# Reordering the opening part of a two-layer conditioned expert kernel: small parameter steps first, some loads later, unread products on TensorE

## The chip, the cores and the metric

The kernel runs on one core of one Trainium2 chip. The metric is device time in microseconds, from one launch to its end. The kernel before took 1190.12 us (median of three runs: 1186.35, 1190.12 and 1195.05). One further execution was recorded by the hardware profiler, and every duration below is from it.

Engines are named as the profile names them: PE is TensorE (its weight loads are listed as PEld), DVE is VectorE, ACT is ScalarE, POOL is GpSimd, and SP is SyncE, which here only issues DMAs. A "q" behind a name (SPq, ACTq) is that engine's instruction queue.

## The reference

The input `x` has 8 sequences (the text calls each of them a batch, b0 to b7) of 512 tokens with 256 channels. Two layers are added to it one after the other.

```python
# layer 0: a small adapter chosen by the batch's language, then a layer norm
h = relu(x @ W1[lang] + b1[lang])                  # 256 -> 64
y = x + h @ W2[lang] + b2[lang]                    # 64 -> 256
c = norm(y) * gamma[lang] + beta[lang]
# layer 0: experts choose tokens
S = softmax(c @ Wg.T).swapaxes(1, 2)               # 8 experts
G, I = top_k(S, 128)                               # 128 of the 512 tokens, per batch and expert
out = G * (gelu(c[I] @ W1 + b1) @ W2 + b2)         # 256 -> 1024 -> 256
x = x + scatter_add(out, I)
# layer 1: causal running means with learned rates (tau) and blend weights, gates, a layer norm
# layer 1: 64 routed experts, 8 per token, and a shared expert; their sum is added to x
```

Two things of layer 1 matter here, because they depend on the parameters alone and not on `x`: the rates `alpha = 1 / (1 + exp(tau))` (9 numbers) and the softmax of the blend weights (256 x 8 numbers). They can be computed at any time before layer 1 begins.

## The kernel before

**How the order comes about.** The function `tile_adaln_ffn_kernel` does not emit instructions as it goes. It adds steps to an `Order`: each step has an engine, a guessed cost in us, a rank, the keys that it reads and writes, and a function that emits its instructions. `Order.run` then plays through these guesses (a table switch of ACT is guessed at 1.3 us, a DMA at 0.19 MB per us) and calls the steps' functions in the order so found; where several steps could begin within 0.25 us of each other, the lower rank goes first. On the chip only the order on each engine remains. Each engine works strictly through its own list, and an instruction waits only for the data and buffers that it really needs. So `after=` or a changed cost sets no wait on the chip: it moves a step in the list. A step that is late holds up everything behind it on its engine.

SP issues nearly all loads. A load on SP waits until the load eight places before it has landed; in the lists this stands as a wait on one of eight DMA semaphores used in turn.

**The opening part**, for each batch b, is `adapter(b)` (line 302):

- loads of the transposed rows (`load_xb`, line 312, tile `axb`, three buffers) and of the rows (`load_xt`, line 317, tile `axt`, three buffers), 512 KB each. For b0 and b1 the rows are loaded from ACT's queue, all others from SP's.
- gathers by POOL of the language's weights (`row_w1` line 324, `row_w2` line 331, tile `aw`, two buffers each) and gains (line 337).
- `down` (PE, line 357, two products of 512 columns), `relu` (ACT, line 360), `up` (PE, line 375, four products of 256 columns over 65 rows; for b2, b3 and b4 the rows themselves are added on PE through an identity, line 379).
- the sum (DVE line 384, or ACT line 390), its statistics (DVE lines 406 and 407, or ACT lines 428 and 434), a square root (ACT line 411 or 441), a reciprocal (DVE line 418 or 445), the norm (ACT line 456), a transposition (PE line 265, ACT line 280), the eight expert scores per token (PE line 472), and their copy (DVE line 481).

After b0 and b1 comes `choose(0)`: softmax, and then 16 rounds of three DVE instructions each (lines 542, 543 and 544), in which one chain of dependent instructions finds the best 128 tokens, eight at a time. Its lists (lines 552 to 573) are what the first experts wait for. `choose(1)` does the same for b2 to b7, later.

Then `expert(n)` runs 32 times (4 pairs of batches, 8 experts): a gather of the tokens (POOL line 612), transposition (PE line 625, ACT line 280), `up` (PE line 646), gelu (ACT line 656), `down` (PE line 713), and a scatter-add (POOL line 731). The weights of an expert are 2 MB (lines 593 and 598, two buffers each). Layer 1 follows pair by pair (`conditioning`, `route`), interleaved with the experts of the next pairs; then the shared expert, and the 64 routed experts.

**The parameter steps** are in `w_rates` (line 770): `less` (DVE 787, 788), `exp_tau` (ACT 773), `exp_blend` (ACT 791), `rates` (DVE 776 to 782) and `shares` (DVE 795 to 797), all of rank 95. Their inputs `taus` and `blend` are loaded in `w_load` (line 747) with the weights of layer 1, rank 30. ACT needs its "exp" table for them, and its "sqrt" table for the norms.

The lines that call these:

```python
nc.scalar.activation(root, eps, AF.Sqrt)           # line 1498: loads ACT's sqrt table
...
w_load()
w_rates()
```

Of the kernel before, what the change touches and what calls it, by code (L numbers as in the profile page):

```python
# [26 lines left out]
PAIR = 2 * 2 * (H // P) * F1 + 3 * H  # L27
FAR = 6
NEAR = 6
LATE = ()  # L30
EPS = 1e-5
NEG = -3.0e38
# [112 lines left out]
def kernel(ctx: ExitStack, tc: tile.TileContext, d: dict, out: bass.AP):  # L145
# [148 lines left out]
    groups = [GROUPS[0], [b for g in GROUPS[1:] for b in g]]  # L294
    lgs = [r0.tile([P, NC // 2, 2, len(g) * E0], F32, name=f"lg{i}") for i, g in enumerate(groups)]

    begun, last_adapter = [], []

    def small(name, shape):
        return r0.tile(shape, F32, name=name)  # L300
# [1 line left out]
    def adapter(b):  # L302
# [1 line left out]
        rank = b if early_one else 50 + b  # L304

        by_dve = early_one or b > 4
        hot = 1.0 if b else 1.7
        xb, xt, w1, w2, hT, xa, c0, c0T = ((k, b) for k in ("axb", "axt", "aw1", "aw2", "ahT", "axa", "ac0", "ac0T"))

        def load_xb():  # L310
# [2 lines left out]

        def load_xt():
            t = tile_of(xt, "axt", [P, NC, H])
            queue = nc.scalar if early_one else nc.sync
            queue.dma_start(out=t, in_=d["x"][b].rearrange("(c p) h -> p c h", p=P))

        def keep():
            nc.sync.dma_start(out=x1_rows[b].rearrange("(c p) h -> p c h", p=P), in_=V[xt])  # L320
# [22 lines left out]
            t = tile_of(hT, "ahT", [A + 1, S])  # L343
            nc.gpsimd.memset(t[A : A + 1, :], 1.0)

        load(512 * KB, load_xb, new=[(xb, "axb")], rank=b)
        load(512 * KB, load_xt, new=[(xt, "axt")], rank=b)
        pool(1.1, row_w1, new=[(w1, "aw1")], rank=rank - 3, lag=2.5)
        pool(1.1, row_w2, new=[(w2, "aw2")], rank=rank - 3, lag=2.5)
        pool(1.0, one, new=[(hT, "ahT")], rank=rank)  # L350
        pool(1.1, row_gains, w=[("gains", b)], rank=rank + 2, lag=2.5)

# [6 lines left out]
        def relu():  # L359
            nc.scalar.activation(V[hT][:A, :], V["ph", b][:A, :], AF.Relu, bias=V[w2][:A, H : H + 1])  # L360

        pe(2.0 * hot, down, r=[w1, xb, w2, hT], new=[(("ph", b), "mm")], rank=rank, after=() if early_one else begun)
        act(0.7, relu, r=[("ph", b), w2], w=[hT], rank=rank)

        sums = ("asum", b)
# [129 lines left out]
    def choose(g):  # L495
        n = len(groups[g])
        rank = 10 if g == 0 else 60
        lg = lgs[g]
        lgr = lg.rearrange("p q h (b e) -> p (q h b) e", e=E0)
        G, R = NC * n, n * E0  # L500
        K = ("choice", g)
        t = {}

        def less():
            t["mx"] = only([P, G], F32, name=f"mx{g}")
            nc.vector.tensor_reduce(t["mx"], lgr, AX.X, ALU.max)
            nc.vector.tensor_tensor(lgr, lgr, t["mx"].unsqueeze(2).to_broadcast([P, G, E0]), ALU.subtract)

        def exp():
            nc.scalar.activation(lgr, lgr, AF.Exp)  # L510

        def share():
            t["sm"] = only([P, G], F32, name=f"sm{g}")
            nc.vector.tensor_reduce(t["sm"], lgr, AX.X, ALU.add)
            nc.vector.reciprocal(t["sm"], t["sm"])
            nc.vector.tensor_tensor(lgr, lgr, t["sm"].unsqueeze(2).to_broadcast([P, G, E0]), ALU.mult)

        def turn():
# [12 lines left out]
        dve(0.8, less, r=[("lg", g, b) for b in groups[g]], w=[K], rank=rank)  # L531
        act(0.35, exp, w=[K], rank=rank, table="e")
        dve(0.9, share, w=[K], rank=rank)
        pe(0.7, turn, r=[K], new=[(("cpt", g), "mm")], rank=rank)
        s = dve(0.5, keep, r=[("cpt", g)], w=[K], rank=rank)
        if g == 0:
            begun.append(s)
        for i in range(K0 // 8):
            def one(i=i):
                prob, best, best_i = (t[k] for k in ("prob", "best", "best_i"))  # L540
                o = slice(8 * i, 8 * i + 8)
                nc.vector.max(best[:, o], prob)
                nc.vector.max_index(best_i[:, o], best[:, o], prob)
                nc.vector.match_replace(prob, best[:, o], prob, -1.0)

            dve(1.45, one, w=[K], rank=rank)


        def lists_of():
            t["lists"] = [only([2 * R, K0], F32, name=f"best{k}{g}") for k in "fbr"]  # L550
            for dst, src in zip(t["lists"], (t["best_i"], t["best_i"][:, ::-1], t["best"][:, ::-1])):
                nc.vector.tensor_copy(dst, src)

        def turn_lists():
            pt = bank(("clt", g))
            for k, src in enumerate((*t["lists"], t["best"])):
                nc.tensor.transpose(pt[:, 2 * R * k : 2 * R * (k + 1)], src, ident[: 2 * R, : 2 * R])

        def keep_lists():
            gT = r0.tile([P, R], F32, name=f"gT{g}")  # L560
            ix = r0.tile([P, R], I32, name=f"ix{g}")
            first_ones = only([P, R], F32, name=f"fo{g}")
            apart = only([P, R], F32, name=f"ap{g}")
            n1, n2, v2, v1 = (V["clt", g][:, R * k : R * (k + 1)] for k in (0, 3, 5, 6))
            held = only([P, 2, R], F32, name=f"hd{g}")
            nc.vector.tensor_copy(held[:, 0], n1)
            nc.vector.tensor_copy(held[:, 1], v1)
            nc.vector.tensor_tensor(first_ones, held[:, 1], v2, ALU.is_ge)
            nc.vector.tensor_tensor(gT, held[:, 1], v2, ALU.max)
# [15 lines left out]
    def expert(n):  # L585
# [16 lines left out]
        def load_3():  # L602
            nc.sync.dma_start(out=tile_of(b2, "fb2", [P, H]), in_=d["fb2"][e : e + 1, :].to_broadcast([P, H]))

        load(1024 * KB, load_1, new=[(w1, "fw1")], rank=20 + n)
        load(1024 * KB, load_2, new=[(w2, "fw2")], rank=20 + n)
        load(128 * KB, load_3, new=[(b2, "fb2")], rank=20 + n)

        which = 0 if bs[0] in groups[0] else 1
        for b in bs:  # L610
# [129 lines left out]

    W = {}

    def w_load():
        def one(name, shape, src, size):
            def fn():
                W[name] = wp.tile(shape, F32, name=name)
                nc.sync.dma_start(out=W[name], in_=src)
            load(size, fn, w=[name], rank=30)

        def one_w(name, k, n):  # L750
            one(name, [P, k // P, n], d[name].rearrange("(c p) n -> p c n", p=P), 4 * k * n)

        one("bn2", [D1, 1], d["bn2"], 32)
        one("cb", [P, 3, NH], d["cb"].rearrange("p (k c) -> p k c", k=3), 3 * KB)
        one("lgb", [P, 2 * NH], d["lgb"], 2 * KB)
        one("taus", [P, 1 + D1], d["taus"].to_broadcast([P, 1 + D1]), 4 * KB)
        one("blend", [P, NH, D1], d["blend"].rearrange("p (c k) -> p c k", c=NH), 8 * KB)
        one("wn2", [P, P], d["wn2"], 64 * KB)
        one("bn1", [P, 1], d["bn1"], 512)
        one_w("wn1", H, P)  # L760
        one_w("lwg", 2 * H, H)
        one_w("wsoma", H, H)
        one_w("wtemp", H, H)
        one_w("wout", H, H)
        one_w("rw", H, E1)
        one_w("wsgu", H, 2 * F1)
        one_w("wsd", 2 * P, H)

    def w_rates():
# [5 lines left out]
        def rates():  # L775
            nc.vector.tensor_scalar_add(W["alpha"], W["alpha"], 1.0)
            nc.vector.reciprocal(W["alpha"], W["alpha"])

            W["hb"] = wp.tile([P, 3, NH], F32, name="hb")
# [16 lines left out]
            nc.vector.reciprocal(W["bmx"], W["bmx"])  # L796
            nc.vector.tensor_tensor(bw, bw, W["bmx"].unsqueeze(2).to_broadcast([P, NH, D1]), ALU.mult)

        dve(0.5, less, w=["blend"], rank=95)
        act(0.3, exp_tau, r=["taus"], w=["alpha"], rank=95, table="e")  # L800
        act(0.3, exp_blend, w=["blend"], rank=95, table="e")
        dve(0.8, rates, r=["cb", "bn2"], w=["alpha", "hb"], rank=95)
        dve(0.8, shares, w=["blend"], rank=95)

        def ranks():
            nc.vector.tensor_copy(early, early_i)
            nc.vector.tensor_copy(early1, early1_i)

        dve(1.1, ranks, w=["early"], rank=96)

    ix_c1 = wp.tile([P, E1], I32, name="ix_c1")

# [682 lines left out]


    last_tokens = []
    nc.scalar.activation(root, eps, AF.Sqrt)
    load(8 * KB, lambda: nc.sync.dma_start(
        out=fwg, in_=d["fwg"].rearrange("(c p) e -> p c e", p=P)), w=["fwg"], rank=0.5)  # L1500
    for b in range(B):
# [7 lines left out]
    w_rates()  # L1509
    last_adapter += order.steps  # L1510
    for n in range(len(units)):
        expert(n)
# [93 lines left out]
```

## Time and profile before

| what | us |
|---|---|
| median of three runs | 1190.12 |
| profiled execution, its time | 1186.26 |
| profiled execution, its span | 1184.5 |
| PE busy (share of the span) | 1035.0 (87%) |
| DVE busy | 684.9 (58%) |
| ACT busy | 490.9 (41%) |
| POOL busy | 379.5 (32%) |
| first product of the program (PE line 357) | at 11.66 |
| first of the 16 rounds of `choose(0)` (DVE line 542) | at 42.58 |
| lists of `choose(0)` ready (DVE line 573) | at 69.52 |
| first transposition for an expert (PE line 625) | at 75.64 |

The profile gives, for a stretch of time, how long each engine was busy, and the clock granted to TensorE as a share of its full speed. [...] A wait is listed with the engine and line that waited, what ended the wait, the total in us, the number of waits, and the longest. The time between the span (1184.5 us) and the execution's own time (1186.26 us) is 1.8 us.

### The profile page before, as it was taken

The page shows a single profiled execution, that of the slowest core. Times are in us where ns is not written, and L with a number is a line of the kernel's source. Part 1 is how long each engine was busy: PE and PEld are TensorE (multiplying, and loading weights), DVE is VectorE, ACT ScalarE, POOL GpSimd, SP SyncE. Part 2 cuts the span into 40 slices and gives each one's busy share as a digit, 9 for nine tenths or more (in the row PEclk, how much of TensorE's full clock was granted, in tenths as well). Part 3 has the DMA queues.
Part 4 walks back from the last instruction along what each step waited for, and adds up shares of the span by engine and source line. Part 5 has one row for each costly group of instructions (what it writes and reads, how often), then busy time and mean ns, then how long its engine had stood idle before and what let it go on. Part 6 is the DMA issues. An engine that isn't in the chain of part 4 may idle for free. (4 is left out here: it accounts for less than half of the span.)

```text
span 1184.5 us, 12863 instructions
## 1 busy us (share of the span) xinstructions
PE 1035.0 (87%) x4261; PEld 757.8 (64%) x4261; DVE 684.9 (58%) x1447; ACT 490.9 (41%) x1016; POOL 379.5 (32%) x305
## 2 busy tenths in 40 slices
PE   5769999999999999999999999999886878778850
PEld 2558888858678767778676877544454555456630
DVE  2532281059892978984898946688857323223323
ACT  1548653443455543536443535433351323223310
POOL 7132133313232313232222212000001566667850
PEclk9669999999999999999999999899997989889995
DMA  8846466677365866456764533941236779777559
GB/s 293 275 159 202 136 187 190 196 236 231 96 207 159 251 202 212 126 153 184 231 203 146 174 94 79 359 146 36 93 125 251 239 202 246 209 210 170 93 104 387
DMA packets 89602, 221.74 MB, mean 187 GB/s; under 512 B 14896, under 2 KB 62488, under 8 KB 77120
## 3 DMA queue, kind: packets, MB, share of 16 engines
q1 hardware_dynamic: 62880, 182.86, 44.4%
q0 software_dynamic: 25600, 37.01, 16.5%
q10 hardware_dynamic: 1056, 1.05, 0.3%
q8 instruction: 34, 0.56, 0.2%
q14 instruction: 32, 0.26, 0.1%
HBM read 177.69 MB, written 47.32 MB: 190 GB/s over the span
## 5 line engine op out<-in xcount | busy, mean ns | idle before, releaser
L646 PE MATMUL hid<-exT,fw 128*128 128x256 f32 x1024 | 230.7, 380 | 3.3 <-ACT hf L656 3.3
L713 PE MATMUL res<-fw,hf 128*128 128x256 f32 x1024 | 232.6, 379 | 0.0
L646 PEld LDWEIGHTS hid<-exT,fw 128*128 128x128 f32 x1024 | 193.3, 191 | 33.2 <-ACT hf L656 4.5
L713 PEld LDWEIGHTS res<-fw,hf 128*128 128x128 f32 x1024 | 191.6, 190 | 25.8 <-issue 1.5
L731 POOL DMA_INDIRECT x_rows<-y,ix x64 | 117.2, 1831 | 231.6 <-ACT y L728 226.4
L612 POOL DMA_INDIRECT xg<-c_rows,ix x64 | 65.8, 1027 | 251.1 <-PE hid L625 220.9
L656 ACT ACTIVATE hf<-hid,fb 128x256 f32<-128x256 f32 x256 | 104.6, 471 | 73.5 <-PE hid L646 73.3
L982 DVE TENSOR_TENSOR_SCAN t<-alpha,u 128x512 f32<-128x512 f32 x84 | 102.8, 1224 | 2.9
L971 DVE SCALAR_TENSOR_TENSOR u<-gx,blend,mdb 128x512 f32<-128x512 f32 x128 | 95.4, 745 | 1.4 <-DMA mdb<-md_rows 0.4
L728 ACT ACTIVATE y<-y,gT 128x256 f32<-128x256 f32 x64 | 32.2, 507 | 141.5 <-DVE y L725 141.4
L1444 DVE COPY xye<-res 128x256 f32<-128x256 f32 x64 | 27.2, 425 | 105.3 <-PE res L1441 102.9
L1398 POOL DMA_INDIRECT xe<-c_rows,ix_c x64 | 63.5, 992 | 56.3 <-DVE ix_c L1285 34.7
L280 ACT ACTIVATE xeT<-mm,lgb 128x128 f32<-128x128 f32 x128 | 50.1, 454 | 45.7 <-PE mm L1407 43.9
L725 DVE TENSOR_TENSOR y<-res,fb 128x256 f32<-128x256 f32 x64 | 26.6, 419 | 68.8 <-PE res L713 68.8
L1420 ACT ACTIVATE xsl<-hid 128x192 f32<-128x192 f32 x64 | 21.1, 330 | 108.7 <-PE hid L1417 108.7
L280 ACT ACTIVATE exT<-hid,gains 128x128 f32<-128x128 f32 x128 | 48.0, 457 | 29.8 <-PE hid L625 29.8
L984 DVE TENSOR_TENSOR tmp<-tmp,t 128x512 f32<-128x512 f32 x84 | 58.1, 692 | 2.9
L1447 POOL DMA_INDIRECT out_dram<-xye,ix_c x32 | 51.0, 1592 | 25.9 <-DVE xhe L1423 11.9
L1417 PE MATMUL hid<-wfar,xeT 128*128 128x384 f32 x144 | 58.3, 533 | 0.0
L1447 POOL DMA_INDIRECT odd<-xye,ix_c x32 | 50.9, 1590 | 23.0 <-issue 12.4
L1435 DVE COPY xheT<-mm 128x256 f32<-128x256 f32 x64 | 27.0, 421 | 46.6 <-PE mm L1432 46.6
L1407 PE MATMUL mm<-ident,xe 128*128 128x128 f32 x128 | 25.5, 297 | 28.8 <-DMA xe<-c_rows,ix_c 28.8
(208 smaller groups left out, 1622.9 us busy)
## 6 DMA issues: line engine op xcount, KB each, us to landing
fw<-in_fw_dram SPq DMA_DIRECT2D x64, 1024.0 KB, 5.5
wfar<-in_wpair_dram SPq DMA_DIRECT2D x18, 1152.0 KB, 5.9
mdb<-md_rows SPq DMA_DIRECT2D x32, 512.0 KB, 5.2
wnear<-in_wpair_dram SPq DMA_DIRECT2D x14, 1152.0 KB, 7.6
axb<-in_xT_dram SPq DMA_DIRECT2D x8, 512.0 KB, 5.8
fb<-in_fb_dram SPq DMA_DIRECT2D x32, 128.0 KB, 4.7
x_rows<-axt SPq DMA_DIRECT2D x8, 512.0 KB, 7.4
c_rows<-ac SPq DMA_DIRECT2D x8, 512.0 KB, 2.8
```

What stands on the lines that cost most here:

```text
L280: nc.scalar.activation(dst, src, AF.Identity, bias=gain[:, NH + hc : NH + hc + 1], scale=gain[:, hc : hc + 1])
L612: nc.gpsimd.indirect_dma_start(out=tile_of(("xg", u, b), "xg", [P, H]), out_offset=None, in_=c0_rows[b], in_offset=bass.IndirectOffsetOnAx ...
L646: nc.tensor.matmul(t[:, i, :], V[w1][:, hc, f * P : (f + 1) * P], V[exT][:, hc, :], start=hc == 0, stop=hc == NH - 1,)
L656: nc.scalar.activation(t[:, i, :], p[:, i, :], AF.Gelu_apprx_tanh, bias=fb1[:, e, f : f + 1])
L713: nc.tensor.matmul(V[res][:, :H], V[hf][:, i, j * K0 : (j + 1) * K0], V[w2][:, f, :], start=f == 0, stop=f == NF - 1,)
L731: nc.gpsimd.indirect_dma_start(out=x1_rows[b], out_offset=bass.IndirectOffsetOnAxis(ap=lists[b][0][:, e : e + 1], axis=0), in_=V[y], in_of ...
L971: nc.vector.scalar_tensor_tensor(u, V[K["gx"]][:, hc, :], W["blend"][:, hc, k : k + 1], V[mdb][:, k % 2, :], ALU.mult, ALU.mult,)
L982: nc.vector.tensor_tensor_scan(t, decay(1 + k), u, 0.0, ALU.mult, ALU.add)
L984: nc.vector.tensor_tensor(whole, whole, t, ALU.add)
L1398: nc.gpsimd.indirect_dma_start(out=tile_of(xe, "xe", [P, H + E1]), out_offset=None, in_=c1_rows, in_offset=bass.IndirectOffsetOnAxis(ap=ix ...
L1417: nc.tensor.matmul(t[:, : 2 * F1], V[xeT][:, hc, :], wgu()[:, hc, :], start=hc == 0, stop=hc == NH - 1)
L1447: nc.gpsimd.indirect_dma_start(out=odd if j else out, out_offset=bass.IndirectOffsetOnAxis(ap=ix_c1[:, e : e + 1], axis=0), in_=V[ye], in_ ...
```

## The change

- The parameter steps come first. `taus` and `blend` are loaded by SP right behind the language numbers; the exp and reciprocal steps get rank -3. ACT loads its exp table at the start, does the two exps, and then loads its sqrt table (the step on `root`). What needs `cb` and `bn2` is split off as `halves`.
- The rows of b0 and b1 (`load_xt`) are issued by SP and no longer by ACT. In the order, the loads of rows of b1 and the rows `axt` of b0 and b1 are put behind the POOL gathers of their language weights; the loads for b2 to b7, and all loads of expert weights, are put behind `down` of b1. The loads of the layer 1 weights (about 2.2 MB, in 13 loads) are not held.
- `warm` adds 28 products of the identity with itself (128 x 128, float32) at the head of PE's list. Nothing reads them.
- Two guessed costs change (`hot`, 1.7 to 1.0 for b0; a round of `choose`, 1.45 to 1.6), which moves steps in the lists.

What this does to the lists: on PE the 28 products come first; `down` of b3 now stands ahead of `up` of b2; and `down` b4, `up` b3, and the transposition and scores of b2 all stand ahead of the transposition of the `choose(0)` lists (line 557 before). Up to then the list of before had, beyond b0 and b1, only `down` b2, `up` b2, and `down` b3 and b4. On SP the order becomes: language numbers, `taus`, `blend`, `axb` of b0, `fwg`, `fb`, the 13 layer 1 loads, `axt` b0, `axb` b1, `axt` b1, a store, `axb` and `axt` of b2, `axb` of b3 and b4, a store, and then the weights of two experts. On DVE the reciprocal of b0 stands ahead of the sums of b1. From the lists of `choose(1)` on, that is for 2062 of PE's 2435 instructions and for the like share of the other engines' lists, the order is the same as before. ACT has 56 table loads in place of 60.

```diff
+WARM = 7
...
+    def warm():
+
+        for k in range(WARM):
+            def idle(k=k):
+                t = bank(("warm", k), "hid")
+                for i in range(4):
+                    nc.tensor.matmul(t[:, i * P : (i + 1) * P], ident, ident, start=True, stop=True)
+
+            pe(0.9, idle, new=[(("warm", k), "hid")], rank=-5)
...
-        hot = 1.0 if b else 1.7
+        hot = 1.0
...
-            queue = nc.scalar if early_one else nc.sync
-            queue.dma_start(out=t, in_=d["x"][b].rearrange("(c p) h -> p c h", p=P))
+            nc.sync.dma_start(out=t, in_=d["x"][b].rearrange("(c p) h -> p c h", p=P))
...
-        load(512 * KB, load_xb, new=[(xb, "axb")], rank=b)
-        load(512 * KB, load_xt, new=[(xt, "axt")], rank=b)
-        pool(1.1, row_w1, new=[(w1, "aw1")], rank=rank - 3, lag=2.5)
-        pool(1.1, row_w2, new=[(w2, "aw2")], rank=rank - 3, lag=2.5)
+        rows = []
+        if b == 0:
+            load(512 * KB, load_xb, new=[(xb, "axb")], rank=b)
+        rows.append(pool(1.1, row_w1, new=[(w1, "aw1")], rank=rank - 3, lag=2.5))
+        rows.append(pool(1.1, row_w2, new=[(w2, "aw2")], rank=rank - 3, lag=2.5))
+
+        if b:
+            load(512 * KB, load_xb, new=[(xb, "axb")], rank=b, after=rows[:1] if b == 1 else first_up)
+        load(512 * KB, load_xt, new=[(xt, "axt")], rank=b, after=rows[1:] if early_one else first_up)
...
+        if early_one:
+            first_up[:] = [s]
...
-            dve(1.45, one, w=[K], rank=rank)
+            dve(1.6, one, w=[K], rank=rank)
...
-        load(1024 * KB, load_1, new=[(w1, "fw1")], rank=20 + n)
+        load(1024 * KB, load_1, new=[(w1, "fw1")], rank=20 + n, after=first_up)
...
-        dve(0.5, less, w=["blend"], rank=95)
-        act(0.3, exp_tau, r=["taus"], w=["alpha"], rank=95, table="e")
-        act(0.3, exp_blend, w=["blend"], rank=95, table="e")
-        dve(0.8, rates, r=["cb", "bn2"], w=["alpha", "hb"], rank=95)
-        dve(0.8, shares, w=["blend"], rank=95)
+        one("taus", [P, 1 + D1], d["taus"].to_broadcast([P, 1 + D1]), 4 * KB, -3)
+        one("blend", [P, NH, D1], d["blend"].rearrange("p (c k) -> p c k", c=NH), 8 * KB, -3)
+        dve(0.5, less, w=["blend"], rank=-3)
+        act(0.3, exp_tau, r=["taus"], w=["alpha"], rank=-3, table="e")
+        exps = [act(0.3, exp_blend, w=["blend"], rank=-3, table="e")]
+        dve(0.4, rates, w=["alpha"], rank=-3)
+        dve(0.6, shares, w=["blend"], rank=-3)
+
+        act(0.2, lambda: nc.scalar.activation(root, eps, AF.Sqrt), rank=-3, table="q", after=exps)
...
-    nc.scalar.activation(root, eps, AF.Sqrt)
+    halves = w_rates()
+    warm()
```

`first_up` is assigned once for b0 and once for b1, and read when the later steps are added; it holds `down` of b1 by then (line 357 before), whatever its name says.

More of the change, by code (lines that the diff above doesn't have):

```diff
@@ L295 @@
     lgs = [r0.tile([P, NC // 2, 2, len(g) * E0], F32, name=f"lg{i}") for i, g in enumerate(groups)]
-    begun, last_adapter = [], []
+    begun, last_adapter, first_up = [], [], []
+    def warm():
[5 more added lines that the diff above has]
+            pe(0.9, idle, new=[(("warm", k), "hid")], rank=-5)
     def small(name, shape):
@@ L360, in relu @@
             nc.scalar.activation(V[hT][:A, :], V["ph", b][:A, :], AF.Relu, bias=V[w2][:A, H : H + 1])
-        pe(2.0 * hot, down, r=[w1, xb, w2, hT], new=[(("ph", b), "mm")], rank=rank, after=() if early_one else begun)
+        s = pe(2.0 * hot, down, r=[w1, xb, w2, hT], new=[(("ph", b), "mm")], rank=rank, after=() if early_one else begun)
+        if early_one:
+            first_up[:] = [s]
         act(0.7, relu, r=[("ph", b), w2], w=[hT], rank=rank)
@@ L603, in load_3 @@
             nc.sync.dma_start(out=tile_of(b2, "fb2", [P, H]), in_=d["fb2"][e : e + 1, :].to_broadcast([P, H]))
-        load(1024 * KB, load_1, new=[(w1, "fw1")], rank=20 + n)
-        load(1024 * KB, load_2, new=[(w2, "fw2")], rank=20 + n)
-        load(128 * KB, load_3, new=[(b2, "fb2")], rank=20 + n)
+        load(1024 * KB, load_1, new=[(w1, "fw1")], rank=20 + n, after=first_up)
+        load(1024 * KB, load_2, new=[(w2, "fw2")], rank=20 + n, after=first_up)
+        load(128 * KB, load_3, new=[(b2, "fb2")], rank=20 + n, after=first_up)
         which = 0 if bs[0] in groups[0] else 1
@@ L741, with one, fn @@
     W = {}
-    def w_load():
[L744 to L748, printed above, removed]
+    def one(name, shape, src, size, rank=30):
+        def fn():
+            W[name] = wp.tile(shape, F32, name=name)
+            nc.sync.dma_start(out=W[name], in_=src)
+        load(size, fn, w=[name], rank=rank)
+    def w_load():
         def one_w(name, k, n):
@@ L755, in w_load @@
         one("lgb", [P, 2 * NH], d["lgb"], 2 * KB)
-        one("taus", [P, 1 + D1], d["taus"].to_broadcast([P, 1 + D1]), 4 * KB)
-        one("blend", [P, NH, D1], d["blend"].rearrange("p (c k) -> p c k", c=NH), 8 * KB)
         one("wn2", [P, P], d["wn2"], 64 * KB)
@@ L777, in rates, with halves @@
             nc.vector.reciprocal(W["alpha"], W["alpha"])
+        def halves():
             W["hb"] = wp.tile([P, 3, NH], F32, name="hb")
@@ L807, in ranks @@
             nc.vector.tensor_copy(early1, early1_i)
-        dve(1.1, ranks, w=["early"], rank=96)
+        dve(1.1, ranks, w=["early"], rank=-2)
+        return halves
     ix_c1 = wp.tile([P, E1], I32, name="ix_c1")
@@ L1508 @@
     w_load()
-    w_rates()
+    dve(0.4, halves, r=["cb", "bn2"], w=["hb"], rank=-2)
     last_adapter += order.steps
```

## The prediction

> **What bounds the kernel now.** I read the page first, then PE by stages, then who waits in the first 80 us, then the instructions there. The page's second part shows the busy tenths in 40 slices of 29.6 us, with the granted TensorE clock below:
>
> ```profile
> PE   5769999999999999999999999999886878778850
> ...
> PEclk9669999999999999999999999899997989889995
> ```
>
> PE is at 9 from the fourth slice to about 830 us; only the first three are thin, and there the clock is low as well. The stages, cut where the clock changes (columns: window, its length, busy us and instructions of PE, PEld, DVE, ACT, POOL, then clock, DMA share, GB/s):
>
> ```profile
> 0.00:26.40 26.40, 12.79 (x24) 6.50 (x24) 5.82 (x22) 3.17 (x6) 18.89 (x31) 1.00 0.90 315
> 26.40:50.25 23.85, 19.94 (x63) 14.65 (x64) 11.82 (x45) 9.72 (x18) 3.10 (x4) 0.50 0.88 295
> 50.25:60.70 10.45, 5.22 (x16) 2.67 (x15) 8.73 (x35) 7.88 (x22) 3.38 (x4) 0.99 0.58 193
> 60.70:80.95 20.25, 12.26 (x43) 9.76 (x44) 8.82 (x43) 5.91 (x15) 5.71 (x6) 0.50 0.48 163
> 80.95:180.00 99.05, 98.91 (x509) 84.91 (x508) 41.22 (x149) 67.00 (x150) 28.02 (x25) 0.98 0.56 172
> ```
>
> From 80.95 us PE never rests (98.91 of 99.05), so the end is set by how much PE work remains then. Ahead of it PE was busy 12.79 + 19.94 + 5.22 + 12.26 = 50.2 us and idle 30.7, and much of the busy time ran at half clock. That is what the change can win. From the lists of `choose(1)` on, the order on every engine is unchanged, so I expect a gain there to pass to the end whole; the later phases wait on work that this stretch delivers. The waits of the first 80 us, and the instructions behind two of them:
>
> ```profile
> DVE axa L384 <- PE mm L375: 16.9, 3, 13.5
> PE mm L557 <- DVE bestb L552: 12.3, 1, 12.3
> PE mm L357 <- DMA aw<-in_cw_dram,ix_w: 11.7, 1, 11.7
> ACT blend L791 <- DVE blend L788: 8.9, 1, 8.9
> ```
> ```profile
> 11.66 3.78 PE L357 MATMUL mm<-axb,aw 128*128 128x512 f32 x4 [11.66 <-DMA aw<-in_cw_dram,ix_w]
> 16.26 3.75 PE L375 MATMUL mm<-aw,ahT 65*128 65x256 f32 x8 [0.82 <-issue]
> 19.80 3.50 PE L357 MATMUL mm<-axb,aw 128*128 128x512 f32 x4
> 24.12 1.97 PE L375 MATMUL mm<-aw,ahT 65*128 65x256 f32 x8 [0.82 <-issue]
> ...
> 68.33 2.06 ACT L456 ACTIVATE ac<-axa,anm,ars 128x256 f32<-128x256 f32 x4
> ```
>
> The same `up` takes 3.75 us at 16.26 and 1.97 at 24.12: the first products run at half speed, though the clock column says 1.00 (it seems to start from 1.00). And ACT stood 8.9 us at the blend exp, waiting for `less`, which lay on DVE behind the 16 rounds; the norm of b2, ready at 57.3, came at 68.33. So b2's transposition and scores, and b3's `up`, fell behind the lists, while PE idled 12.3 us.
>
> **The change, part by part.** Times are from the start of the span.
>
> *First products.* POOL's gather for b0 begins at 6.18 as before. It landed after 5.5 us behind 3 MB of rows; the expert tokens at 69.8 landed in 2.7 at best with DMA nearly free. Bounds 8.9 and 11.7; with 0.8 MB in flight I take 10.4. The 28 products: 28 x 128 columns are 3.5 times the 1024 of one `down`, so 3.5 x 3.5 = 12 us cold, 6 warm. They start near 1.5. The clock rose 3.9 to 7.6 us after unbroken work began (46.37 to 50.25; 16.26 to 23), so rise at 5.4 to 9.1 and end at 9.5 to 11.3: cover is the gather, and at worst they delay it by 0.9. I take 10.6 for `down` b0. Warm: `down` 1.75, relu 0.8, `up` 1.97, `down` b1 1.75, relu 0.8, `up` 1.97 = 9.0, to 19.7; before 11.66 to 26.09. The chain on (sums, 2.1 of statistics, root, norm b0; evacuations 1.63; root, norm b1, which no longer waits behind DVE's reversed order) puts norm b1 at 23.95 where it was at 31.17: 7.2 us.
>
> A rule speaks here. The Trainium skill, "TensorE: Matmul & The Clock Gate", "What's actually happening", has the clock fall only after an idle window of about 3.4 us. The row: it fell at 26.4 although PE idled at most 0.8 us at a time in 22.95 to 26.40; that window was 2.32 busy of 3.45, mostly with products of 65 rows. By the rule the clock stays up through the scores (norm to lists two us shorter): 9.2 us. By the row it is lost somewhere in 14 to 20; from nothing lost to 3.7 for `down` and `up` of b1, I take 1.5. So 5.7 us, lists' transposition at 35.8 for 41.5.
>
> *Loads.* `axt` b0 goes from ACT at 0.91 to SP behind the 13 layer 1 loads. The skill's "DMA: Bandwidth & Descriptors", "Issuing engines are not separate DMA queues", says that the issuing engine matters only for issue time: two issues of about 0.5 us. The row that speaks against it is SP's own waits in the first 34 us:
>
> ```profile
> SPq L747 <- DMA fw<-in_fw_dram: 9.4, 4, 2.7
> ```
>
> SP waits for the load eight places back. Those are now small ones, not 1 MB of expert weights. At 0.46 us an issue, `axt` b0 issues at 9.6, `axb` b1 at 10.1; 3.8 MB at the 360 GB/s of the windows from 3 us is 14 to 14.5. Needed: 14.2 and 15.2. By the rule no cost; the row bounds it at 16 us (the same loads took 14.69 to 30.9). I take 0.3, within the rounding. Expert weights start near 16; needed from 79.
>
> *Parameter steps.* Nine DVE instructions of 0.1 to 0.2 and two ACT exps of 0.2 move into DVE's wait of 13.5 and ACT's of 13.2; cover gone, they'd cost 1.3 plus one table load (1.28). The 8.9 us stall goes. What is late next: the reciprocal of b2 now stands after 8 rounds of 1.475 on DVE. From the lists' transposition: two `down`s to 6.4 (before one, 3.9), `up` b2 to 9.9, sums 10.8, squares 13.1, table and root 14.7; DVE is there at 12.3. It stands 2.5 us, before 1.1: +1.4. The rounds, and PE's `up` b4 behind them, wait for it.
>
> *The hole.* While DVE does the rounds, PE now does `down` b4 and `up` b3 (to 15.3), transposition and scores of b2 (to 23.5). Continuous work starts with `up` b4 at 35.8 + 26.2 + 1.4 + 0.4 = 63.8, before at 69.0: 5.2. Already done by then and not before: `up` b3 3.45, transposition 1.0, scores 1.85 = 6.3 (warm prices; row 103.88 to 109). Loss after the start: before, cold until 80.95, about 5.9, plus 1.1 of waits; now cold until the clock rises 3.4 to 6.8 into it, 2.55. Difference 4.45. Sum 5.2 + 6.3 + 4.45 = 15.95.
>
> Against that, ACT now has sums, squares, norms of b3 to b5, evacuations and gelus, about 27 us in 32. Following the list, PE waits for the evacuation of b5's transposition (1 to 1.5), of b6's (about 0.8) and little else. Bounds 0 (as in 80.95 to 180) and 8; I take 2.5.
>
> Gain 13.4: the profiled execution's 1186.3 (span 1184.5 and 1.8 around it) becomes 1172.9. That execution lies at the low end of the four known (1186.26, 1186.35, 1190.12, 1195.05; middle 1188.2); for a median I set 1188.2 - 13.4 = **1174.8**, in round 1175.
>
> **The rivals.**
>
> *The clock falls before the first products* (0.18). A microsecond or so of idle between the unread products and `down`, and 65-row work after: for, the fall at 26.4; against, the clock stayed through 53.7 to 57.1 with 1.77 of 3.4 busy. The first part wins 2.2, not 5.7: 1178.5.
>
> *The clock holds through the scores* (0.12), as the rule has it: 3.5 better, 1171.
>
> *The hole only moves* (0.13): ACT becomes the bound after the lists, PE waits 8 in place of 2.5: 1180.5. For: two norms, six evacuations ahead of the first gelu. Against: ACT was busy 17 of 20 us at 80 to 100 and PE did not wait.
>
> *The rows of b1 come late* (0.07), the slower side. If each of the 13 waits from `lgb` to `axb` b1 costs what the lone loads were apart at 15 to 26 us, about 2.7, `axb` b1 issues at 39 and lands at 45: `down` b1 29.5 late, 16 more than the gain, 1204. It decides from `down` b1 at 29. Against: the loads eight back are a tenth as big.
>
> *The forecast* holds 0.50, within 4 us either way: 1171 to 1179.
>
> **How the numbers follow.** Range: 1171 less the spread of the executions (about 4) is 1167; above, the moved hole with the same spread and part of the late rows, 1186. Within 1% is what a measurement of this kernel can hardly tell from no change; 1% is 11.9 us, so 1178.2. Faster by more: 0.4 of the forecast, 0.08, 0.12 and 0.02 of the next three, 0.62. Slower by more: 0.05, all late rows. Same: 0.33.
>
> **What the profile after should show.** `down` b0 near 10.6 at about 0.44 us an instruction; `axt` b0 landing by 14.5; first round near 36.9; no ACT wait at the blend exp, one DVE wait of 2 to 3 us within the rounds; scores of b2 done before the lists; `up` b4 straight behind the lists' transposition near 63.8; PE without waits over 2 us after that. Wrong if `down` b1 starts past 18, if PE idles over 5 us after 64, or if the later stages give the gain back.

## The result and the profile after

The kernel after takes 1177.78 us (median of 14 runs, 1172.21 to 1183.14); the kernel before took 1185.97 in the runs beside it, so the medians lie 8.2 us apart. The ratio is 0.9924, with a 95% interval of 0.9901 to 0.9946; of 1185.97 us that is 9.0 us less, and by the interval 6.4 to 11.7 (it is not the quotient of the two medians). Timed again beside the last experiments, the same kernel gave 0.9928 (0.9903 to 0.9952). The time lies inside the range of the forecast, 2.8 us above its number, and the gain is two thirds of the 13.4 us that were added up. It is a gain of less than 1%, to which the forecast gave 0.33, against 0.62 for a larger one.

The profiled execution took 1173.81 us with a span of 1172.0. Its page, PE's busy tenths and the granted clock in 40 slices of 29.3 us:

```profile
PE   7889999999989999989999999999886888678850
...
PEclk8779999999999999999999999999997999899985
```

PE is filled from the first slice on (7, 8, 8 for 5, 7, 6), partly with the unread products. The clock is still low in the first three slices (8, 7, 7; before 9, 6, 6). The waits of PE and of DVE in the first 90 us (who waited, for whom; us in total, times, longest):

```profile
PE mm L372 <- DMA gains<-in_cgb_dram,ix_w: 5.4, 1, 5.4
PE mm L574 <- DVE bestb L569: 3.9, 1, 3.9
```
```profile
DVE axa L401 <- DMA axt<-in_x_dram: 11.8, 1, 11.8
...
DVE ars L462 <- ACT asd L458: 1.2, 1, 1.2
```

PE's hole ahead of the lists of `choose(0)` is 3.9 us, before 12.3; ACT's stall of 8.9 us at the blend exp is gone. In their place stands something new: DVE sits 11.8 us until the rows `axt` of b0 are there, and PE sits 5.4 us ahead of `down` of b1. The name of that second releaser (`gains`) is only the event that came last; a later execution of the same kernel, shown below, names the rows. PE in order of time (start, us, line, operands, idle time before it):

```profile
10.63 1.88 PE L372 MATMUL mm<-axb,aw 128*128 128x512 f32 x4
13.33 1.96 PE L392 MATMUL mm<-aw,ahT 65*128 65x256 f32 x8 [0.82 <-issue]
20.74 3.75 PE L372 MATMUL mm<-axb,aw 128*128 128x512 f32 x4 [5.44 <-DMA gains<-in_cgb_dram,ix_w]
25.31 1.97 PE L392 MATMUL mm<-aw,ahT 65*128 65x256 f32 x8 [0.82 <-issue]
...
41.07 0.58 PE L538 MATMUL mm<-ident,lg 128*32 128x128 f32 x2 [1.92 <-DVE lg L533]
...
67.52 0.28 PE L574 MATMUL mm<-ident,bestf 32*128 32x32 f32 x1 [3.87 <-DVE bestb L569]
...
68.06 1.22 PE L392 MATMUL mm<-aw,ahT 65*128 65x256 f32 x2
```

`down` of b0 is warm at 10.63. But `down` of b1 starts at 20.74, later than the 19.80 of before, and cold (3.75 for 1.88). So the lists' transposition of `choose(0)` (the first line at 41.07; PE line 521 before, 538 after) comes at 41.07, where before had it at 41.51: the faster first products brought 0.4 us there. The gain of this pair was made behind that point.

How much of it reaches the end is read from one marker that both lists have in the same place: the first transposition of layer 1's rows (PE line 265 before, 266 after). Before, and then after:

```profile
238.34 1.06 PE L265 MATMUL mm<-ident,xr 128*128 128x128 f32 x8 [0.30 <-DMA xr<-x_rows]
```
```profile
228.24 1.06 PE L266 MATMUL mm<-ident,xr 128*128 128x128 f32 x8 [0.61 <-DMA xr<-x_rows]
```

It starts 10.1 us earlier. The same distance is found at the transpositions that before has at 406 and at 590 us (10.1 at both). Between 655 and 745 us before then lost about 3 us more, by its clock (0.96 and 0.94, against 1.00); that is not put down to the change, since the last experiments find this fall in one execution and not in another. The opening's 10.1 is one pair of executions; it lies inside the interval of the timed gain.

### The profile page after: what moved, and what is told of

The parts are those of the page before. It is cut to its first block, busy times and chain, and to the rows that moved or that the text cites. A ratio compares the mean times of both kernels' runs of the same rounds, so it can differ in the third digit from the quotient of the medians.

```text
span 1172.0 us, 12980 instructions
## 1 busy us (share of the span) xinstructions
PE 1029.4 (88%) x4317; PEld 758.2 (65%) x4317; DVE 685.1 (58%) x1447; ACT 486.6 (42%) x1012; POOL 379.7 (32%) x305
## 5 line engine op out<-in xcount | busy, mean ns | idle before, releaser
L281 ACT ACTIVATE exT<-hid,gains 128x128 f32<-128x128 f32 x128 | 48.1, 457 | 29.3 <-PE hid L642 29.3
L1440 PE MATMUL hid<-wfar,xeT 128*128 128x384 f32 x144 | 54.7, 505 | 0.0
```

Of the source, the lines that this page charges most:

```text
L281: nc.scalar.activation(dst, src, AF.Identity, bias=gain[:, NH + hc : NH + hc + 1], scale=gain[:, hc : hc + 1])
L1440: nc.tensor.matmul(t[:, : 2 * F1], V[xeT][:, hc, :], wgu()[:, hc, :], start=hc == 0, stop=hc == NH - 1)
```

## The experiments

All compute the full result; those without unread products leave out only these. "Marker" is the start of that first transposition of layer 1's rows in the profiled execution; lists' transposition, PE's hole ahead of the lists, and the first work behind them are read from PE in order of time, as above.

| kernel | `down` b1 | lists' transposition | PE's hole | first work behind lists | marker | ratio (95%) |
|---|---|---|---|---|---|---|
| before | 19.80 | 41.51 | 12.3 | 68.97 | 238.3 | 1 |
| after | 20.74 | 41.07 | 3.9 | 68.06 | 228.2 | 0.9924 (0.9901 to 0.9946) |
| after, again | 20.29 | 42.10 | 3.7 | 68.84 | 231.2 | 0.9928 (0.9903 to 0.9952) |
| rows ahead of weights | 15.17 | 33.79 | 1.9 | 60.26 | 222.6 | 0.9862 (0.9828 to 0.9896) |
| no unread products | 20.30 | 42.11 | 5.0 | 68.72 | 228.3 | 0.9916 (0.9879 to 0.9954) |
| both of these | 15.87 | 34.55 | 0.5 | 60.96 | 220.6 | 0.9889 (0.9844 to 0.9934) |
| rows on ACT's queue | 21.19 | 41.42 | 5.2 | 68.25 | 227.8 | 0.9953 (0.9932 to 0.9975) |
| rows first, on ACT's queue | 14.55 | 38.76 | 3.9 | 66.26 | 226.2 | 0.9896 (0.9858 to 0.9935) |
| before + parameter steps | 18.41 | 39.13 | 13.7 | 65.44 | 236.1 | 1.0000 (0.9975 to 1.0026) |
| after - early parameter steps | 20.19 | 41.89 | 3.8 | 69.52 | 229.6 | 0.9933 (0.9905 to 0.9962) |
| before, rows on SP | 17.23 | 37.08 | 12.8 | 63.41 | 232.9 | 0.9993 (0.9965 to 1.0022) |
| after, one small load on ACT | 19.95 | 39.28 | 3.9 | 66.40 | 227.5 | 0.9962 (0.9932 to 0.9993) |

The openings of single executions differ by some us, but one reading of the table does not depend on them. From the lists' transposition to the marker, the three kernels with before's order on PE take 195.9 to 197.0 us, and the nine executions with the new order 186.0 to 189.1, whatever their loads, parameter steps and unread products. So 6.8 to 11.0 us are won behind the lists in every comparison, and the timed 9.0 lies in the middle of that. Ahead of the lists nothing is won as long as the rows come late: their transposition is at 39.3 to 42.1 in those six executions, and at 37.1 to 41.5 in the three of before's kind.

**Rows ahead of the weights.** The suspicion after the result: `axt` of b0 and `axb` of b1 were late because ten loads of layer 1 weights stood ahead of them on SP. Here these ten are issued behind the store of b1's norm; all other engines keep their lists.

```diff
+    HELD = ("wn2", "bn1", "wn1", "lwg", "wsoma", "wtemp", "wout", "rw", "wsgu", "wsd")
...
-            nc.sync.dma_start(out=W[name], in_=src)
+            if name in HELD:
+                held.append((name, src))
+            else:
+                nc.sync.dma_start(out=W[name], in_=src)
...
+            if b == 1:
+                for name, src in held:
+                    nc.sync.dma_start(out=W[name], in_=src)
```

> The changed kernel with one difference: ten of the layer 1 weight loads (2.2 MB) leave their place ahead of the rows of b0 and b1 on SP and follow the store of b1's norm; the lists of all other engines are those of the changed kernel. Theory (the weights ahead on SP are what made the rows late): rows of b0 land by about 9 us, transposed rows of b1 by about 11, down of b1 starts straight behind up of b0 near 15.2 (in the changed kernel 20.74) and warm; first round of the search near 37 to 38 (changed: near 42); up of b4 near 64 (68.06); first transposition of layer 1's rows near 223.5 to 224.5 (228.24; before 238.34); ratio to before near 0.988. Rival (POOL's gathers and gains, named in the wait of the trace, hold down of b1): down of b1 stays within 1.5 us of 20.7, that transposition stays at 227 to 229, ratio 0.992.

SP's issues of the rows in the kernel after, and then in this one (start, us of issue):

```profile
11.15 0.47 SPq L327 DMA_DIRECT2D axt<-in_x_dram  x1
12.61 0.34 SPq L323 DMA_DIRECT2D axb<-in_xT_dram  x1
```
```profile
5.12 0.38 SPq L327 DMA_DIRECT2D axt<-in_x_dram  x1
5.54 0.51 SPq L323 DMA_DIRECT2D axb<-in_xT_dram  x1
```

They go out 6 to 7 us earlier, and PE in this kernel shows what follows:

```profile
13.37 1.97 PE L392 MATMUL mm<-aw,ahT 65*128 65x256 f32 x8 [1.56 <-ACT ahT L375]
15.17 1.88 PE L372 MATMUL mm<-axb,aw 128*128 128x512 f32 x4
17.87 1.97 PE L392 MATMUL mm<-aw,ahT 65*128 65x256 f32 x8 [0.82 <-issue]
```

`down` of b1 follows `up` of b0 without a wait and warm. The lists' transposition comes at 33.79, 7.3 us earlier than in the kernel after, the marker 5.7 earlier, and the timed median is 1174.16 (beside 1188.35 of before): the fastest of these kernels by its median, with an interval (0.9828 to 0.9896) wholly below that of the kernel after. The forecast had `down` of b1 at 15.1, the lists' transposition at 35.8 and the work behind the lists at 63.8; with the rows in time they are at 15.17, 33.79 and 60.26. So the forecast went wrong at the rows; behind them its chain was 2.0 to 3.5 us too slow.

**No unread products.** `WARM` goes from 7 to 0, in the kernel after and in the one with the rows first.

```diff
-WARM = 7
+WARM = 0
```

> The changed kernel without its 28 unread products; all else in the same order. Theory (the rows come at 19.3 and 20.7 whatever PE does, so the warm clock is spent in that wait): down and up of b0 take 3.8 and 3.8 us instead of 1.9 and 2.0, down of b1 still starts near 20.7, the first transposition of layer 1's rows stays at 227.5 to 229, ratio to before 0.992. Rival (the unread products are what wins): that transposition 3.5 us or more later, 231.5 to 233, ratio 0.995.

> Both differences together: the weights behind the rows, and no unread products. With the rows early, the half clock is no longer hidden: down b0 3.8, up b0 3.8, down b1 3.5, up b1 2 to 3.8, against 1.9, 2.0, 1.8 and 2.0 to 3.8 with them. Theory: first transposition of layer 1's rows 4 to 6 us later than with the weights held and the unread products kept, near 228 to 230, ratio 0.992 to 0.993. Rival (PE's start has no part in it, the chain runs over other engines): within 1.5 us of it.

In the first, `down` of b0 starts earlier (8.27) and cold, and all the same ends far ahead of the rows. The marker is 228.3 for 228.2: the unread products bought nothing that shows in the kernel after. They even held up `down` of b0: without them it began 2.4 us earlier than in this execution of the kernel after, and 1.0 earlier than in the second (9.26). With the rows in time I expected to lose 4 to 6 us without them, and that fell. PE in that kernel:

```profile
9.47 3.78 PE L372 MATMUL mm<-axb,aw 128*128 128x512 f32 x4 [9.47 <-DMA aw<-in_cw_dram,ix_w]
14.07 1.97 PE L392 MATMUL mm<-aw,ahT 65*128 65x256 f32 x8 [0.82 <-ACT ahT L375]
15.87 1.88 PE L372 MATMUL mm<-axb,aw 128*128 128x512 f32 x4
```

Only `down` of b0 is cold (3.78 us, 1.88 warm); at `up` of b0, 4.6 us later, the clock is up. With the products `up` of b0 started at 13.37, held by `relu`; without, at 14.07. That is 0.7 us, and the lists' transposition keeps it (33.79 and 34.55). At the marker this kernel is even 2 us ahead (220.6 for 222.6), mostly because the other one was granted a lower clock from 84 to 104 us (0.83 for 0.91); between the two timed ratios the intervals decide nothing.

**The parameter steps.** Alone, on the kernel before; and taken out of the kernel after (rank 95 and the old place, with the rest of the change kept). The first:

```diff
-        dve(0.5, less, w=["blend"], rank=95)
-        act(0.3, exp_tau, r=["taus"], w=["alpha"], rank=95, table="e")
-        act(0.3, exp_blend, w=["blend"], rank=95, table="e")
+        dve(0.5, less, w=["blend"], rank=-3)
+        act(0.3, exp_tau, r=["taus"], w=["alpha"], rank=-3, table="e")
+        exps = [act(0.3, exp_blend, w=["blend"], rank=-3, table="e")]
```

> The kernel before with the parameter steps alone moved to the front (and taus and blend loaded first); loads, guessed costs and PE's head as before. Theory (the work that fills PE's wait comes from the loads' new order, not from these steps): ACT's 8.9 us wait is gone and the norm of b2 is done early, but its transposition and scores still stand behind the lists on PE, so only its wait for the norm (about 2 us) is won; first transposition of layer 1's rows at 235 to 237 (before 238.34, changed 228.24), ratio 0.998. Rival (the ACT wait was the loss): that transposition at 229 to 231, ratio 0.993.

The second is the same lines the other way round, on the kernel after.

> The changed kernel with its parameter steps back at rank 95 and their loads among the layer 1 weights; loads, costs and unread products as changed. In the lists the exps now fall between the two relus of b0 and b1, and PE's list still has up of b3 and the scores of b2 ahead of the lists. Theory: two more table loads (2.6 us) lie beside the wait for the rows of b1 and cost 0 to 2 us; first transposition of layer 1's rows at 228 to 230.5, ratio 0.992 to 0.994. Rival (early parameter steps are what opens the hole): at 235 or later, ratio 0.997 or more.

In the first, ACT's stall of 8.9 us is gone, but PE's hole is not. A wait of PE in the first 90 us of that kernel:

```profile
PE mm L557 <- DVE bestb L552: 13.7, 1, 13.7
```

The ratio is 1.0000. In the second the hole is closed though the steps have their old rank:

```profile
PE mm L574 <- DVE bestb L569: 3.8, 1, 3.8
```

Its ratio, 0.9933, cannot be told from 0.9924. (With the loads in their new order the exps come at 17 us, ahead of the rounds, by the list itself.) So the stall was not what kept PE idle. PE's own list was: `up` of b3, the transposition and the scores of b2 stand ahead of the lists in every kernel of the table that gains, and behind them in the three of before's kind. No kernel changed this list alone.

Which lines of the change give PE this list can be played through with `Order.run`, which needs no chip. Without the `after=` on the rows of b0 and b1, all three steps fall behind the lists, as before. Without the holds on the later rows and the experts (`first_up`), or with the two old guesses of cost, `up` of b3 and the transposition stay ahead and only the scores fall behind. So the order that fills the hole comes from placing the rows of b0 and b1 late, which is also what makes them late on the chip; the first experiment keeps the one without the other. None of these other lists was run.

**The rows on ACT's queue.** The rows of b0 and b1 go back to ACT's queue, as before; in the kernel after, and in the one with the rows first.

```diff
-            nc.sync.dma_start(out=t, in_=d["x"][b].rearrange("(c p) h -> p c h", p=P))
+            queue = nc.scalar if early_one else nc.sync
+            queue.dma_start(out=t, in_=d["x"][b].rearrange("(c p) h -> p c h", p=P))
```

> The changed kernel with the rows of b0 and b1 again issued by ACT, the layer 1 weights still ahead of the transposed rows of b1 on SP. Theory (place in SP's list, not the issuing engine): rows of b0 land by about 7 and its sum starts near 14.3 instead of 19.36, but down of b1 still waits for its transposed rows, near 19 to 20; first transposition of layer 1's rows at 226 to 228, ratio 0.991. Rival (the move of the rows from ACT to SP is the loss): down of b1 near 15 to 16, that transposition near 223.5, ratio 0.988.

> The kernel with the weights behind the rows, and the rows of b0 and b1 issued by ACT between its table loads in place of SP. Theory (the issuing engine matters only through the place in the list): transposed rows of b1 issue one place earlier; down of b1 still near 15.2 since up of b0 sets it; first transposition of layer 1's rows at 221 to 224.5, ratio 0.986 within 0.003. Rival (a launch that uses ACT's DMA queue loses some 3 us later: the profile of before and of the run with ACT's queue both lost 3 us more than the others between 564 and 745): that transposition the same, the one at about 730 3 us later than with SP alone, ratio 0.989 or more.

In the first the rows of b0 come in time (the sum of b0 starts at 14.6 for 19.36), but `axb` of b1, still on SP behind the weights, does not. PE there:

```profile
21.19 3.64 PE L373 MATMUL mm<-axb,aw 128*128 128x512 f32 x4 [5.88 <-DMA axb<-in_xT_dram]
```

So of the two late loads it is the transposed rows of b1 that hold the chain, and the marker does not move (227.8 for 228.2). In the second `down` of b1 is 0.6 us earlier than with SP, yet the marker is 3.6 later, at 226.2 where I had expected 221 to 224.5. The place is one evacuation of b0's transposition on ACT, whose releaser the profile names only as "remote":

```profile
27.02 0.78 ACT L281 ACTIVATE ac0T<-mm,gains 128x512 f32<-128x512 f32 x1 [4.89 <-remote]
```

What that was stays open. By their ratios the two were also 3.4 and 4.0 us slower than their twins with the rows on SP (the intervals overlap), and both profiles, like that of before, had a clock of 0.96 between 655 and 700 us where the kernel after had 1.00. Three further runs asked whether the queue does that: the kernel after unaltered, the same with one small load (`fwg`) on ACT, and before with its rows on SP.

```diff
-    load(8 * KB, lambda: nc.sync.dma_start(
+    load(8 * KB, lambda: nc.scalar.dma_start(
```
```diff
-            queue = nc.scalar if early_one else nc.sync
-            queue.dma_start(
+            nc.sync.dma_start(
```

> The changed kernel unaltered, as the measure for the next two on the same chip. Both theories: ratio 0.992 (0.990 to 0.9945), first transposition of layer 1 about 10 us earlier than before.

> The changed kernel with one 8 KB load (the expert scores' weights, needed only after 22 us) issued from ACT's queue and no longer from SP's. My theory: a load on ACT's queue costs nothing in itself, and the 3 us by which the two kernels with rows on ACT's queue were slower came from the clock's falls by chance: ratio as for the changed kernel on this chip, within 0.0015. Rival: any use of ACT's queue costs about 3 us late in the run: ratio 0.0025 to 0.003 higher, and a clock of about 0.96 between 655 and 745 us where the changed kernel had 1.00.

> The kernel before with the rows of b0 and b1 issued from SP and nothing else changed (the other engines' lists stay). My theory: two issues of half a us on SP, nothing on the path (the first product waits for its gather to 11.7): ratio 1.000, within 0.0015. Rival: leaving ACT's queue alone wins about 3 us late in the run: ratio 0.997.

The windows 655 to 700 and 700 to 745 us (window, length, busy us of PE, PEld, DVE, ACT, POOL, then clock, DMA share, GB/s), of the kernel after unaltered, and of the one with a small load on ACT:

```profile
655.00:700.00 45.00, 41.87 (x196) 34.49 (x195) 35.01 (x63) 20.87 (x43) 10.20 (x6) 1.00 0.55 157
700.00:745.00 45.00, 42.34 (x182) 32.40 (x181) 31.03 (x78) 23.51 (x39) 6.21 (x4) 0.96 0.48 154
```
```profile
655.00:700.00 45.00, 42.07 (x189) 34.59 (x189) 29.85 (x59) 20.13 (x42) 7.05 (x4) 1.00 0.42 117
700.00:745.00 45.00, 42.34 (x172) 29.25 (x171) 34.66 (x93) 22.28 (x37) 6.21 (x4) 1.00 0.61 206
```

The late fall of the clock came without ACT's queue (0.96, first fence) and stayed away with it (second fence); before with its rows on SP had 0.96 in both windows, before with the parameter steps, its rows on ACT, 1.00 in both. So the fall does not follow the queue. The medians of the first two are 1178.95 and 1179.07, while their ratios to before stand 0.0034 apart with overlapping intervals; before with its rows on SP is at 0.9993. So what I expected of the small load (a ratio within 0.0015) did not come: the ratio is about as the rival had it, while the medians and the clock are not. All three kernels with a load on ACT's queue stand about 0.003 above their twins, and before gains nothing by leaving that queue. A price of 3 us for the queue is neither shown nor ruled out.

## Why the prediction was right and where it failed

**Loads: the step that failed.** I took `axt` of b0 and `axb` of b1 to land at 14 to 14.5 us, from 3.8 MB at 360 GB/s from 3 us on, and charged 0.3 us for it. They were issued at 11.15 and 12.61 (9.6 and 10.1 in the prediction) and used at 19.36 and, in the unaltered kernel's second execution, at 20.29, where PE's line names its releaser:

```profile
20.29 3.75 PE L372 MATMUL mm<-axb,aw 128*128 128x512 f32 x4 [6.37 <-DMA axb<-in_xT_dram]
```

The windows of the kernel after show which factor was wrong:

```profile
0.00:10.00 10.00, 8.63 (x51) 8.63 (x52) 3.06 (x17) 3.20 (x5) 7.88 (x18) 1.00 0.54 131
10.00:20.00 10.00, 4.47 (x20) 2.64 (x18) 0.64 (x2) 0.68 (x1) 7.71 (x10) 0.89 1.03 348
```

In the first 10 us the DMA engines moved 131 GB/s, 1.3 MB, not the 2.5 MB that the forecast's rate makes from 3 to 10 us. But for `axb` of b0 the loads issued in the first 7 us were small ones, at about half a us each and with waits for the load eight places back; the first weight of 512 KB (`lwg`) is issued only at 7.05. My own sum had the issues at 9.6 and 10.1 beside a full rate from 3 us, and these two don't fit together: what isn't issued isn't moved. As an estimate from these two rates, the missing 1.2 MB are 3.4 us at 348 GB/s, and `axt` of b1, issued at 13.37 and in flight beside the two, is another 0.5 MB, 1.5 us; together about the 5 us by which 19.3 lies behind 14.25. The first experiment confirms the cause: rows ahead of the weights, and the chain is 7.3 us earlier at the lists' transposition. The rule on issuing engines from the Trainium skill ("DMA: Bandwidth & Descriptors", "Issuing engines are not separate DMA queues") is not what failed here: before with its rows on SP stays at 0.9993, and in the kernel after, the place in SP's list is what costs. The three kernels with a load on ACT's queue leave some doubt on it, as said.

**First products: the time met by luck, the worth wrong.** `down` of b0 came at 10.63 (10.6) and warm, but not for the reason given. The prediction let it wait for the gather that POOL begins at 6.18. That is `row_w2`, which `relu` needs; `down` needs `row_w1`, begun at 4.48, and without the unread products it started at 8.27. So the products themselves held it, until 10.63 here and 9.26 in the second execution. (Beside it a sum is off: 16.26 to 23 is 6.7 us, not 7.6.) The 5.7 us at the lists became 0.4, since `down` of b1 had no rows until 20.74: I had it at 15.1, and had named "past 18" as a sign of being wrong. In the wait of 5.44 us the clock that the 28 products had raised was lost again. Here row and rule agree (the Trainium skill, "TensorE: Matmul & The Clock Gate", "What's actually happening": it falls after an idle window of about 3.4 us); with waits of 1.56 us at most, as in the first experiment, it stayed up through `up` of b1. In the scores behind that they part again, and the row decides: there the clock fell although PE idled 0.43 us at most at a time. PE in that kernel:

```profile
22.96 3.08 PE L492 MATMUL mm<-fwg,ac0T 128*128 128x8 f32 x14 [0.28 <-ACT ac0T L281]
25.89 1.95 PE L266 MATMUL mm<-ident,ac 128*128 128x128 f32 x8
```

The eight products of the second line take 1.04 us when warm (73.72 in the kernel after).

And with the rows in time the warm clock was worth 0.7 us in one pair of profiles, where the forecast had 3.5 between its first part with it and without it (5.7 and 2.2). The 3.5 came from before's profile, in which `up` of b0 is still cold (3.75 at 16.26). In the four other executions that begin without unread products it is warm. Two of them are before with the parameter steps, and before with its rows on SP:

```profile
16.60 1.97 PE L375 MATMUL mm<-aw,ahT 65*128 65x256 f32 x8 [0.82 <-issue]
```
```profile
15.43 1.97 PE L374 MATMUL mm<-aw,ahT 65*128 65x256 f32 x8 [0.82 <-issue]
```

So in those four only `down` of b0 was left to win. And with the unread products, `relu` of b0 waited for its own gather. ACT in the first experiment's kernel:

```profile
12.58 0.68 ACT L375 ACTIVATE ahT<-mm,aw 64x512 f32<-64x512 f32 x1 [5.14 <-DMA aw<-in_cw_dram,ix_w]
```

`down` of b0 had ended at 11.80, and this wait, which I had not listed, took about 0.7 us of what it gained.

**Parameter steps: gone as described, with no gain of their own that shows.** The stall left. DVE's wait at the reciprocal of b2 is 1.23 us, where I had 2.5: the root was done 14.1 us after the lists' transposition (14.7), and DVE came to it after 12.9 (12.3). The prediction tied the closing of the hole to the blend exp; the two runs with and without the steps untie it.

**The hole.** In the profiled pair, against before's opening, and by the terms of the prediction: continuous work starts at 68.06 for 68.97, 0.9 (forecast 5.2: the lists' transposition came 5.3 later than forecast, and the way from it to this work was 1.0 shorter, chiefly by the 1.3 us that DVE did not wait). Work already done by then: 6.3, taken over from the forecast; `up` b3, the transposition and the scores of b2 stand ahead of the lists. Clock: cold from 68.06 to about 72.4, by the rows 1.22, 1.06, 1.06, 1.06 and 0.95 us for pairs that take 0.6 warm, a loss of 2.35 for before's 7.0, so 4.65 (4.45). PE's waits after that, from the window of the kernel after (columns as above):

```profile
80.95:180.00 99.05, 97.96 (x503) 85.61 (x502) 41.56 (x146) 55.74 (x119) 31.19 (x26) 0.98 0.57 176
```

PE was busy 97.96 of 99.05 us, in the same stretch of before 98.91: 0.95 more idle (forecast 2.5). Sum: 0.9 + 6.3 + 4.65 - 0.95 = 10.9; the marker says 10.1, and 0.8 is not accounted for. The forecast's 13.4 less the missing 4.3 of the start, plus 1.55 of waits that did not come and 0.2 of clock, is 10.85, the same sum.

**The rivals.** That the clock falls before the first products is not seen: `down` of b0 is warm. That it holds through the scores is not seen either: in the kernel after the transposition of b1 takes 1.95 us at 33.17, and it was cold with the rows in time as well (above). The rows of b1 coming late was the rival that named the right place, with a size that was too large: I had it from `down` b1 at 29, and it came at 20.74. Its mechanism, waits of SP ahead of the issue, holds in part: `axb` of b1 was issued at 12.61, 2.5 us later than forecast and not at 39, and the rest of its delay is bytes in flight. Its price was about 4.3 us of gain rather than a loss. That ACT becomes the bound, or that the later stages give the gain back, is not seen: the distance is 10.1 us at 238, 406 and 590 us.

**Why the forecast was right in sign and range all the same.** Two terms carry the gain, 6.3 us of work moved into the hole and 4.65 us of cold clock avoided. Both came from rows of the profile before, and the work that they name is found in its new place. The one that failed took a third of the gain away. That the number came within 2.8 us is in part luck. In the profiled pair the way to the lists' transposition brought 0.4 us for 5.7 forecast, and the way from there to the marker 9.7 for 7.7, so two errors lay against each other. And 1175 was counted down from 1188.2, while before took 1185.97 in these runs, 2.2 us less.

## What to carry to other kernels

Before a load is moved in an in-order queue, sum the bytes that can be in flight at each time from the issue times, and not from a rate that holds when the queue is full; and then look at which of the moved loads is first needed by the chain. A stall that disappears is worth only what the engine that sets the end does with the time: ask what stands next in its own list. Raising the clock ahead of work helps only if that work has its data when the clock is up.

## What the runs showed of the hardware

One program's opening differs from execution to execution by more than I had thought. The kernel after had its marker at 228.2 in one and at 231.2 in the other, with `up` of b1 warm (1.97) and cold (3.75); and three kernels whose first products are those of before had `down` of b1 at 19.80 cold, 18.41 warm and 17.23 warm. At the marker, before with its rows on SP is 5.4 us ahead of before, and its ratio is 0.9993. So up to five us between the openings of two single profiles say nothing by themselves here, and the profile of before, to which the sum was made, had the slowest of these three. The clock also falls for a while late in the run, in some executions and not in others of the same kernel (the kernel after had 1.00 in one and 0.96 in the other from 700 to 745 us). What such a fall costs can be read between two later transpositions of layer 1's rows, near 585 and near 735 us: before, with 0.96 from 655 us on, takes 153.4 us between them, and the kernel after, with 1.00 from 655 to 700, takes 150.3 in both executions.
